# Two sequences' rotation sums, norm products and softmax scalings moved from GpSimd to VectorE, with every engine's order replanned

## The chip, the cores and the metric

The kernel runs on one core of one Trainium2 chip. Its engines are named as the profile names them: PE is TensorE (matmuls; PEld are its weight loads), DVE is VectorE, ACT is ScalarE, POOL is GpSimd, SP is SyncE, which issues most of the DMAs. Each engine works through its own instructions in the order in which they stand in its queue; semaphores make one engine wait for another. PSUM holds matmul results, SBUF everything else on the chip. The metric is the time of one execution in microseconds (us): the median of the runs shown. A line such as L1158 is a line of the kernel before; in the changed kernel lines behind L424 stand three lines higher.

## The reference

The input is eight sequences of 256 tokens with 128 channels. It goes through eight layernormed residual sublayers: an RG-LRU recurrence, local attention with a feed-forward (two depth layers), Mamba, a top-1 mixture of 32 experts, chunked attention, a top-2 mixture of 8 experts, typed attention with 16 heads, and a ternary linear layer. The change touches the second, local attention. For one depth layer, cut to what matters:

```
x = x + attention(shift_token(x));  x = x + ffn(layernorm(shift_token(x)))
def l2norm(t): return t / clip(norm(t, axis=-1), 1e-12)
def rotate_half(x): x1, x2 = split(x, 2); return concatenate([-x2, x1])
q, k, v = heads(shift_token(x) @ wqkv)              # 8 heads of 64
q, k = l2norm(q) * q_scale, l2norm(k) * k_scale
q = q * cos * scale + rotate_half(q) * sin * scale
k = k * cos / scale + rotate_half(k) * sin / scale
sim = 8 * q @ k^T                 # windows of 64, one window looked back, causal
out = softmax(sim) @ v;  attention = out @ wo
```

A rotation is thus a sum of two products with tables; the norm's reciprocal multiplies q and k; and a softmax row is divided by its sum.

## The kernel before

**Stages.** The program runs six stages one behind the other: rglru, local_mamba, moe1, chunked, moe2, typed. local_mamba (L1335) holds the local attention and the Mamba layer. `one_sequence(b)` (L1383) runs a sequence through two local blocks, adds the residual (L1388) and normalizes. `interleave` (L1470) keeps up to four sequences open at once; when sequence b is finished, `mamba_sequence` (L1223) of the same sequence follows. Its state update is, eight times for each sequence, a product (L1304), a scan (L1306) and a product (L1307) on DVE. The second group of RG-LRU sequences (4 to 7, `rglru_group`, L1005) runs beside the first local blocks, with a reciprocal (L1035), a scan (L1040) and products (L1042, L1043) on DVE and its sigmoids and exponentials on ACT.

**A local block.** `local_block` (L1172) makes the shifted input h (copies L1069 on POOL), calls the attention and then the feed-forward (L1186 to L1218). `local_qk` (L1073) computes for q (n = 0) and k (n = 1) two tiles of 128 tokens each:

- PE multiplies h with the weights into a PSUM bank `qk`; ACT squares it into `qsq` (L1085); DVE sums the squares by head into `ss` (L1086).
- DVE forms the two rotation products t1 and t2 from PSUM (L1090, L1092; 128x512 each), with the scales folded into the tables.
- POOL clips ss from below (L1097), ACT turns it into the reciprocal norm rn by a logarithm and an exponential (L1098, L1099).
- POOL adds t2 to t1 (L1105) and, for k alone, multiplies with rn (L1107). PE transposes the result into `qkt` (L1110) and ACT copies it out. For q the norm is applied later, as a scale within the softmax.

`local_attention` (L1119) then works on two halves of 128 tokens: PE writes the scores `sc`; DVE takes the negated maximum nm (L1147) and multiplies it with q's rn (L1148); ACT computes eight exponentials with their sums (L1153); DVE takes the reciprocal rc of the sums (L1157); POOL multiplies e with rc (L1158, 128x1024); PE transposes e into `pt` (L981), ACT and DVE copy it to `ptsb` (L983), and PE multiplies with v into `o`, after which `wo` follows.

**What sets the order.** A class `_Order` (L312) plans all instructions of the program before it is built. It has a table `LENGTHS`, which gives for each form of instruction the time it keeps its engine and the time until its result is there; a table `BIAS` of corrections in ns to an instruction's priority, by engine, tile name and stage (stages are numbered 1 to 6, so "DVE nm 2" is the nm operations of local_mamba on DVE); and `STAY`, which holds back an instruction that would make PE change its tile group or ACT its function table. `plan` (L612) walks through time and on each engine issues the ready instruction with the lowest corrected start; it also models that DVE and POOL operations of some forms exclude each other. `impose` (L760) then writes the result into the program as order on every engine:

```
for ring in order.values():
    for a, b in zip(ring, ring[1:]):
        self.tc.add_manual_dep(...)
```

So the order on PE, DVE, ACT, POOL and SP, in all stages, follows from these tables together with the instructions.

Of the kernel before, what the change touches and what calls it, by code (L numbers as in the profile page):

```python
# [18 lines left out]
ALU = mybir.AluOpType  # L19
# [4 lines left out]
P = 128  # L24
# [287 lines left out]
class _Order:  # L312
# [14 lines left out]
    STAY = dict(PE=80, ACT=740)  # L327
    BIAS = {
        "ACT  1": 100, "ACT  5": 585, "ACT bt 3": 5, "ACT bt 5": -775, "ACT d 2": -425, "ACT da 2": -45, "ACT e 2": -5, "ACT e 4": 965, "ACT e 6": -20,
        "ACT got 3": 575, "ACT h 2": -200, "ACT ix 4": 15, "ACT k 2": 265, "ACT lavp 2": 210, "ACT lnrs 1": -10, "ACT lnrs 2": -160, "ACT lnsq 1": -135,  # L330
        "ACT lnsq 2": 15, "ACT ot 2": 10, "ACT ptsb 2": -595, "ACT ptsb 6": -515, "ACT q 2": 20, "ACT qsq 2": 10, "ACT r 2": -5, "ACT rg 1": 10,
        "ACT rg 2": -915, "ACT rn 2": 15, "ACT rs 4": 340, "ACT rs 6": -690, "ACT s 6": 200, "ACT sakq 2": -10, "ACT sg 3": -550, "ACT sh 5": -2525,
        "ACT spe 1": -220, "ACT spt 1": -50, "ACT st 6": 100, "ACT sz 2": 280, "ACT v 2": 885, "ACT vs 4": 320, "ACT xchunked 2": 15, "ACT xs 2": -610,
        "DVE biasfull 3": -335, "DVE biaspart 3": -20, "DVE bt 5": -5, "DVE c 1": 590, "DVE centre 0": 320, "DVE d 2": 10, "DVE decaypart 4": -600,
        "DVE e 4": 570, "DVE four 4": 100, "DVE fs 4": -70, "DVE gate 4": 340, "DVE get 2": 200, "DVE got 4": 530, "DVE identb 0": -50, "DVE k 6": 500,
        "DVE lg 2": 2240, "DVE lo 4": -265, "DVE mv 4": -660, "DVE mv 5": 100, "DVE mv 6": -485, "DVE nm 2": -3975, "DVE nm 6": 4960, "DVE nth 4": -45,
        "DVE oh 2": -725, "DVE oh 5": -10, "DVE ptsb 2": -3895, "DVE ptsb 6": 895, "DVE put 4": -395, "DVE put 5": 55, "DVE q 5": -825, "DVE q 6": -475,
        "DVE rc 2": -1225, "DVE rc 6": 10, "DVE route 2": -55, "DVE s 5": 10, "DVE sares 2": 70, "DVE sel 2": -1590, "DVE sg 3": -140, "DVE sm 4": 2720,
        "DVE spl 1": -215, "DVE ss 2": 370, "DVE st 4": 85, "DVE st 6": 1645, "DVE sum 4": 170, "DVE t 2": 440, "DVE u 2": 250, "DVE vs 4": 50,
        "DVE we 4": 1425, "DVE xc 2": 460, "DVE xla 4": -15, "DVE xlocal 2": -5, "DVE xmoe 5": -200, "DVE xmoe 6": -580, "DVE xpf 4": -370,  # L340
        "DVE xrglru 2": 120, "DVE xsa 4": 80, "DVE z 4": -1990, "PE a 2": -100, "PE acc 5": 155, "PE b 2": -35, "PE bt 3": 75, "PE bt 5": 50,
        "PE cum 2": -995, "PE cum 4": -25, "PE cum 5": -615, "PE fold 2": 2915, "PE g 2": -4155, "PE gate 2": 785, "PE kps 4": 135, "PE less 2": 295,
        "PE lg 2": 1680, "PE lg 4": 50, "PE ln 2": -10, "PE o 2": 10, "PE o 6": -10, "PE pg 5": 150, "PE ps 4": -15, "PE pt 4": -130, "PE pu 3": 220,
        "PE py 3": -200, "PE py 5": 170, "PE qk 2": 25, "PE qkt 2": -720, "PE raw 2": -8675, "PE rows 2": 400, "PE sc 2": -50, "PE sc 4": 65, "PE sc 6": 5,
        "PE v 5": 290, "PE vps 2": 4075, "PE vps 4": 25, "PE wo 2": 75, "PE wo 6": -85, "PE wout 2": -115, "PE xin 2": 1180, "PE xps 2": -2540, "PE y 2": 20,
        "PE z 2": -450, "PE zt 5": 560, "PE zt 6": 25, "POOL d 2": 130, "POOL e 6": -30, "POOL got 4": -200, "POOL h 2": 370, "POOL k 5": 400,
        "POOL k 6": 850, "POOL km 6": 1240, "POOL mean 0": 1510, "POOL places 5": -200, "POOL q 6": 20, "POOL rest 4": -65, "POOL rg 1": -800,
        "POOL rg 2": -200, "POOL rot 2": -400, "POOL s 6": -750, "POOL t 2": 550, "POOL zero 0": -655, "POOL zeros 1": 385, "SP bc 2": -970, "SP cst 3": 5,
        "SP got 3": 355, "SP got 5": 350, "SP rottable 0": 80, "SP rows 4": 210, "SP rowschunked 4": -105, "SP vec 0": -830, "SP w 0": 15, "SP w 3": 115,
        "SP wattn 2": 585, "SP wffn 2": 705, "SP wlocal 0": 1175, "SP wmoe 4": 520, "SP xs 2": -105, "SP ybuf 5": -200,  # L350
    }
    LENGTHS = {
        "ACT  LoadActFuncSet  ": (1178, 1283), "ACT d Ln 128x512 128x512": (535, 640), "ACT da Exp 128x255 128x255": (398, 503),
        "ACT e Abs 128x256 128x256": (460, 565), "ACT e Exp 128x128 128x128": (420, 525), "ACT e Exp 128x256 128x256": (461, 566),
        "ACT e Exp 128x512 128x512": (527, 632), "ACT four Exp 128x2 128x2": (100, 205), "ACT got DMACopy 128x512 128x512": (454, 3611),
        "ACT h TensorCopy 64x255 64x255": (295, 400), "ACT lnrs Exp 128x256 128x256": (315, 420), "ACT ot TensorCopy 128x512 128x512": (486, 591),
        "ACT qsq Square 128x512 128x512": (494, 599), "ACT r Relu 128x256 128x256": (460, 565), "ACT rg Exp 128x1020 128x1020": (1039, 1144),
        "ACT rg Exp 128x1024 128x1024": (998, 1103), "ACT rg Ln 128x1024 128x1024": (950, 1055), "ACT rn Exp 128x16 128x16": (110, 215),
        "ACT rn Ln 128x16 128x16": (112, 217), "ACT rs Exp 128x2 128x2": (96, 201), "ACT rs Ln 128x2 128x2": (98, 203),
        "ACT sh Silu 128x512 128x512": (492, 597), "ACT v TensorCopy 128x512 128x512": (485, 590), "ACT xc Identity 128x256 128x256": (460, 565),  # L360
        "ACT xc Silu 128x512 128x512": (526, 631), "ACT xchunked TensorCopy 128x256 128x256": (263, 368), "ACT xmoe Identity 128x256 128x256": (404, 509),
        "ACT xs TensorCopy 33x256 33x256": (257, 362), "ACT xsq Square 128x128 128x128": (297, 402), "DVE biaspart TensorCopy 96x256 96x256": (197, 282),
        "DVE decay TensorScalarPtr 128x512 128x512": (508, 593), "DVE decaypart TensorCopy 128x512 128x512": (331, 416),
        "DVE four TensorScalarPtr 128x4 128x4": (76, 160), "DVE ge TensorScalarPtr 128x256 128x256": (380, 465),
        "DVE ge TensorScalarPtr 85x256 85x256": (372, 457), "DVE got TensorScalarPtr 128x128 128x128": (258, 343),
        "DVE h TensorTensor 128x256 128x256": (312, 397), "DVE hs TensorScalarPtr 128x1024 128x1024": (2189, 2274),
        "DVE hs TensorTensor 128x1024 128x1024": (1116, 1201), "DVE mv BNStatsAggregate 128x2 128x6": (82, 167),
        "DVE nm TensorTensor 128x8 128x8": (66, 151), "DVE ptsb TensorCopy 128x512 128x512": (589, 674), "DVE rc Reciprocal 128x16 128x16": (160, 245),
        "DVE rc Reciprocal 128x4 128x4": (84, 169), "DVE rc Reciprocal 128x8 128x8": (106, 191), "DVE rg TensorScalarPtr 128x256 128x256": (577, 662),
        "DVE rg TensorTensor 128x1024 128x1024": (1109, 1194), "DVE rottable TensorScalarPtr 128x256 128x256": (261, 346),  # L370
        "DVE s TensorScalarPtr 128x128 128x128": (247, 332), "DVE s TensorTensor 128x256 128x256": (323, 408),
        "DVE sm TensorReduce 128x16 128x512": (593, 678), "DVE ss TensorReduce 128x8 128x512": (594, 679), "DVE st BNStats 128x6 128x128": (197, 282),
        "DVE sum TensorReduce 128x32 128x448": (810, 895), "DVE t TensorScalarPtr 128x256 128x256": (384, 469),
        "DVE t TensorTensor 128x512 128x512": (593, 678), "DVE vec TensorTensor 128x1 128x1": (59, 144), "DVE vec TensorTensor 85x1 85x1": (59, 144),
        "DVE vs TensorCopy 128x512 128x512": (594, 679), "DVE wlocal TensorScalarPtr 128x682 128x682": (481, 566),
        "DVE x TensorScalarPtr 128x256 128x256": (368, 453), "DVE xc TensorScalarPtr 128x254 128x254": (383, 468),
        "DVE xc TensorScalarPtr 128x255 128x255": (384, 469), "DVE xla TensorScalarPtr 128x256 128x256": (442, 527),
        "DVE xlocal TensorTensor 128x256 128x256": (311, 396), "DVE xpf TensorScalarPtr 128x256 128x256": (562, 647),
# [393 lines left out]
class _Kernel:  # L772
# [293 lines left out]
    def shift(self, dst, src):  # L1066
# [3 lines left out]
        nc.gpsimd.memset(dst[64:P, 0:1], 0.0)  # L1070
        nc.scalar.copy(dst[64:P, 1:S], src[64:P, 0 : S - 1])

    def local_qk(self, l, h, w, rot, work, local, small, pools):  # L1073


        nc = self.nc
        ss = small.tile([P, 4, 8], F32, tag="ss", name="ss")
        rn = small.tile([P, 4, 8], F32, tag="rn", name="rn")
        ts = []
        for n in range(2):  # L1080
# [31 lines left out]
            if n:  # L1112
                k = dst
# [1297 lines left out]
```

## Time and profile before

| | us |
|---|---|
| median of 3 runs (lowest to highest) | 1642.47 (1641.91 to 1643.14) |
| the profiled execution | 1644.68 |
| its span | 1642.9 |

The granted clock of TensorE over the span was 0.942. By milestones in the timeline of the profiled execution: the first RG-LRU group ends at 41 us; sequence 0's first block (last addition L1218) ends at 121.2 and its second at 211.8; its residual addition (L1388) stands at 213.3 and its first Mamba scan (L1306) at 252.7. L1388 of the eight sequences stands at 213.3, 287.9, 368.4, 446.6, 526.6, 598.7, 659.5 and 719.5 us, that is 60 to 81 us apart. The last scan is at 787.4. The first mixture of experts follows, the chunked stage runs from about 850 to 1262, the second mixture of experts to about 1445 and the typed stage to the end.

How to read the lines that follow. A group line names line, engine, operation, output tile and inputs, partitions x elements and the count; behind the bar the busy time of the group in us and the mean of one instruction in ns; behind the next bar the idle time of the engine just before these instructions and who ended it. A line of waits names the waiting engine, tile and line, then the releaser, then us in total, times and the longest. A line of a stretch names its start and end. Busy time of pipelined instructions overlaps: two DVE operations of 680 ns that follow each other start 600 ns apart.

### The profile page before, as it was taken

What the parts mean: (1) busy time and instruction counts of PE and PEld (TensorE: products, weight loads), DVE (VectorE), ACT (ScalarE), POOL (GpSimd) and SP (SyncE); (2) the same over time, 40 slices, a digit from 0 to 9 for tenths busy, and PEclk for the clock granted to TensorE, in tenths of its full rate; (3) what the DMA queues carried; (4) which work ended last, traced back from release to release, by engine and by line L of the source; (5) the groups of instructions that cost most, each with busy time, mean ns of one, the idle gap of its engine ahead of it and who ended that gap; (6) DMA issues with size and microseconds to landing.
All of it is one profiled execution on the core that took longest, in us unless ns stands there. A gap on an engine that the chain in (4) does not pass through costs nothing. (4 is left out here: it accounts for less than half of the span.)

```text
span 1642.9 us, 28581 instructions
## 1 busy us (share of the span) xinstructions
PE 1417.4 (86%) x10826; PEld 909.4 (55%) x10826; DVE 1102.3 (67%) x2182; ACT 968.6 (59%) x2656; POOL 587.5 (36%) x535
## 2 busy tenths in 40 slices
PE   2688998989898887777579999999998899899997
PEld 1354554545554544334366766777675576556664
DVE  5745568898989898698545557554546333279886
ACT  3777888787978869446125545455453222167775
POOL 1334544535462523101431222212212102467774
PEclk7789999989999999779789999999998899999998
DMA  5000012121212223155430000000000130000000
GB/s 199 1 1 1 1 40 65 40 60 45 65 40 65 53 52 91 52 179 189 151 119 1 8 12 11 10 5 8 32 18 24 46 121 26 26 9 8 5 8 11
DMA packets 45113, 77.97 MB, mean 47 GB/s; under 512 B 5580, under 2 KB 21988, under 8 KB 43824
## 3 DMA queue, kind: packets, MB, share of 16 engines
q1 hardware_dynamic: 39648, 70.02, 14.0%
q0 software_dynamic: 3216, 5.07, 1.1%
q8 instruction: 85, 1.39, 0.4%
q10 hardware_dynamic: 2112, 1.05, 0.2%
q14 instruction: 52, 0.43, 0.1%
HBM read 66.87 MB, written 10.76 MB: 47 GB/s over the span
## 5 line engine op out<-in xcount | busy, mean ns | idle before, releaser
L870 PE MATMUL y<-hs,ident 128*128 128x512 f32 x256 | 139.7, 659 | 35.9 <-DVE hs L1307 35.6
L1158 POOL TENSOR_TENSOR e<-e,rc 128x1024 f32<-128x1024 f32 x32 | 78.0, 2437 | 202.7 <-DVE rc L1157 194.3
L1306 DVE TENSOR_TENSOR_SCAN hs<-da,hs 128x1024 f32<-128x1024 f32 x64 | 149.1, 2331 | 0.2
L2259 ACT ACTIVATE e<-sc,nm 128x128 f32<-128x128 f32 (+1 forms) x256 | 105.2, 427 | 46.6 <-DVE nm L2254 40.3
L1153 ACT ACTIVATE e<-sc,nm,rn 128x128 f32<-128x128 f32 x256 | 114.3, 466 | 13.8 <-DVE nm L1148 13.5
L981 PE MATMUL pt<-ident,e 128*128 128x128 f32 x768 | 114.2, 278 | 9.4 <-POOL e L1158 4.9
L1302 ACT ACTIVATE da<-d,na 128x255 f32<-128x255 f32 x256 | 109.3, 504 | 17.5 <-DVE hs L1306 13.7
L1836 POOL TENSOR_TENSOR e<-e,rc 128x512 f32<-128x512 f32 x32 | 34.0, 1064 | 219.8 <-DVE rc L1835 154.2
L981 PEld LDWEIGHTS pt<-ident,e 128*128 128x128 f32 x768 | 88.5, 141 | 42.5 <-issue 16.1
L2262 POOL TENSOR_TENSOR e<-e,rc 128x1024 f32<-128x1024 f32 x48 | 90.8, 1896 | 39.1 <-DVE rc L2261 32.1
L1105 POOL TENSOR_TENSOR t<-t,t 128x512 f32<-128x512 f32 x64 | 83.9, 1316 | 58.0 <-DVE t L1092 51.6
L1811 ACT COPY kp<-kps 128x512 f32<-128x512 f32 x128 | 74.7, 583 | 49.0 <-PE kps L870 46.4
L1658 POOL DMA_INDIRECT got<-ybuf,get x48 | 45.7, 952 | 159.2 <-DMA ybuf<-ys 97.1
L870 PEld LDWEIGHTS y<-hs,ident 128*128 128x128 f32 x256 | 48.5, 205 | 82.5 <-DVE hs L1307 54.2
L1304 DVE TENSOR_TENSOR hs<-u,bc 128x1024 f32<-128x1024 f32 x64 | 84.3, 1328 | 2.9 <-POOL u L1291 2.9
L1307 DVE TENSOR_TENSOR hs<-hs,bc 128x1024 f32<-128x1024 f32 x64 | 80.6, 1260 | 0.0
L1847 ACT COPY vs<-vps 128x512 f32<-128x512 f32 x64 | 37.4, 585 | 67.1 <-PE vps L870 53.6
L983 DVE COPY ptsb<-pt 128x512 f32<-128x512 f32 x104 | 68.8, 675 | 11.6 <-PE pt L981 9.3
L870 PE MATMUL qk<-w_local,h 128*128 128x512 f32 x128 | 69.3, 631 | 7.5 <-DVE t L1092 7.1
L870 PE MATMUL vps<-sa_vp,x_lf 128*32 128x512 f32 x512 | 68.4, 594 | 0.0
L1847 DVE COPY vs<-vps 128x512 f32<-128x512 f32 x64 | 43.3, 682 | 37.2 <-PE vps L870 25.1
L2057 DVE TENSOR_TENSOR sh<-sh,pu 128x512 f32<-128x512 f32 x32 | 22.0, 688 | 67.1 <-PE pu L870 54.0
(380 smaller groups left out, 3782.4 us busy)
## 6 DMA issues: line engine op xcount, KB each, us to landing
bc<-xs SPq DMA_DIRECT2D x128, 256.0 KB
w_moe<-in_e_dram SPq DMA_DIRECT2D x16, 768.0 KB
w_attn<-in_w_dram SPq DMA_DIRECT2D x4, 1024.0 KB
w_local<-in_w_dram SPq DMA_DIRECT2D x2, 1557.0 KB
places<-zeros SPq DMA_DIRECT2D x2, 1280.0 KB
got<-places SPq DMA_DIRECT2D x6, 256.0 KB
ybuf<-ys SPq DMA_DIRECT2D x8, 160.0 KB
x_in<-in_x_dram SPq DMA_DIRECT2D x1, 1024.0 KB
```

The costliest lines, as they stand in the source:

```text
L870: return self.nc.tensor.matmul(out, lhsT, rhs, start=start, stop=stop)
L981: self.last = self.nc.tensor.transpose(pt[:, j * P : (j + 1) * P], src[:, j * P : (j + 1) * P], self.ident)
L1105: nc.gpsimd.tensor_add(t1, t1, t2)
L1153: nc.scalar.activation(e[:, j, g, :], scs[:, j, g, :], AF.Exp, bias=nm[:, j, g : g + 1], scale=rq[:, j, g : g + 1], accum_out=sm[:, j, g : ...
L1158: nc.gpsimd.tensor_tensor(e, e, rc.unsqueeze(3).to_broadcast([P, 2, 4, P]), ALU.mult)
L1302: nc.scalar.activation(da[:, n, c, 1:S], d[:, c, 1:S], AF.Exp, scale=na[:, i : i + 1])
L1304: nc.vector.tensor_tensor(hs, u.unsqueeze(1).to_broadcast(shp), bn, ALU.mult)
L1306: nc.vector.tensor_tensor_scan(line(hs), line(da), line(hs), 0.0, ALU.mult, ALU.add)
L1307: nc.vector.tensor_tensor(hs, hs, cn, ALU.mult)
L1847: i = copy(v[:, c, :, :].rearrange("p a b -> p (a b)"), ps)
L2259: nc.scalar.activation(e[:, i, :], sc[:, i, :], AF.Exp, bias=nm[:, i : i + 1], accum_out=sm[:, i : i + 1])
L2262: nc.gpsimd.tensor_tensor(e, e, rc.unsqueeze(2).to_broadcast([P, n, keys]), ALU.mult)
```

## The change

`local_qk`, `local_attention` and `local_block` take the engine `eng` as an argument; `one_sequence` passes VectorE for sequences 0 and 1 and GpSimd for the other six. Three operations are issued on that engine: the rotation sum (4 in a block), k's product with the norm (2) and the scaling of the exponentials (2). With two blocks for a sequence that makes 32 instructions. The clipping of ss (L1097) and the copies of h stay on POOL.

The planner's tables are changed as well: `STAY` goes from 80 to 150 for PE and from 740 to 950 for ACT; nearly all entries of `BIAS` have other values, some are gone and some new; `LENGTHS` has newly measured values, mostly a few ns apart, with some entries dropped. Since the order on every engine follows from these, it is another one in all stages.

```diff
-    STAY = dict(PE=80, ACT=740)
+    STAY = dict(PE=150, ACT=950)
     BIAS = {
...
-    def local_qk(self, l, h, w, rot, work, local, small, pools):
+    def local_qk(self, eng, l, h, w, rot, work, local, small, pools):
...
-                nc.gpsimd.tensor_add(t1, t1, t2)
+                eng.tensor_add(t1, t1, t2)
                 if n:
-                    nc.gpsimd.tensor_tensor(t1, t1, rn[:, 2 + t, :].unsqueeze(2).to_broadcast([P, 8, 64]), ALU.mult)
+                    eng.tensor_tensor(t1, t1, rn[:, 2 + t, :].unsqueeze(2).to_broadcast([P, 8, 64]), ALU.mult)
...
-    def local_attention(self, l, h, w, rot, work, local, small, pools):
+    def local_attention(self, eng, l, h, w, rot, work, local, small, pools):
...
-        q, k, rn = yield from self.local_qk(l, h, w, rot, work, local, small, pools)
+        q, k, rn = yield from self.local_qk(eng, l, h, w, rot, work, local, small, pools)
...
-            nc.gpsimd.tensor_tensor(e, e, rc.unsqueeze(3).to_broadcast([P, 2, 4, P]), ALU.mult)
+            eng.tensor_tensor(e, e, rc.unsqueeze(3).to_broadcast([P, 2, 4, P]), ALU.mult)
...
-    def local_block(self, l, x, w, rot, work, local, small, pools):
+    def local_block(self, eng, l, x, w, rot, work, local, small, pools):
...
-        ot = yield from self.local_attention(l, h, w, rot, work, local, small, pools)
+        ot = yield from self.local_attention(eng, l, h, w, rot, work, local, small, pools)
...
-                    x = yield from self.local_block(l, x, w, rot, work, local, small, pools)
+                    x = yield from self.local_block(nc.vector if b < 2 else nc.gpsimd, l, x, w, rot, work, local, small, pools)
```

Of `BIAS`, some entries of the stage of the edit are these (before, then after): "DVE nm 2" -3975, -2300; "DVE ptsb 2" -3895, -6115; "DVE rc 2" -1225, -2400; "PE qkt 2" -720, -6440; "PE raw 2" -8675, -7230; "POOL t 2" 550, 2725; "POOL h 2" 370, 1290.

## The prediction

> **What bounds the kernel now.** I read the busy sums first, then busy time by stretch, then the costliest groups of the early stretch, and last its waits.
>
> ```profile
> PE 1417.4 (86%) x10826; PEld 909.4 (55%) x10826; DVE 1102.3 (67%) x2182; ACT 968.6 (59%) x2656; POOL 587.5 (36%) x535
> ...
> 42.00:120.00 78.00, 57.29 (x313) 34.10 (x312) 48.08 (x82) 56.03 (x135) 23.88 (x28) 0.80 0.00 1
> 120.00:253.00 133.00, 117.13 (x815) 71.63 (x814) 81.27 (x140) 107.94 (x303) 70.51 (x79) 0.99 0.04 13
> 253.00:660.00 407.00, 353.04 (x2020) 209.01 (x2019) 365.02 (x445) 331.38 (x868) 178.90 (x146) 0.97 0.22 58
> 660.00:796.00 136.00, 97.29 (x398) 52.38 (x396) 108.58 (x119) 64.68 (x134) 27.77 (x20) 0.84 0.48 162
> 860.00:1262.00 402.00, 393.31 (x4508) 278.60 (x4500) 226.87 (x722) 196.92 (x461) 84.56 (x92) 1.00 0.04 11
> 1445.00:1620.00 175.00, 170.93 (x1574) 102.85 (x1572) 149.66 (x360) 126.84 (x579) 126.38 (x80) 1.00 0.02 6
> ```
>
> The first line is the whole span. The others are stretches: start and end, length, then busy time (instructions) of PE, weight loads, DVE, ACT and POOL, the granted clock, DMA share and GB/s. The sums hide four regimes. 42–253 holds the first three sequences of local blocks, the two edited ones among them: PE 73%, then 88%; DVE is busy 129.4 of 211 us and idle 81.6. From 253 to 660 the Mamba scans run and DVE is the bound (365.0 of 407). After 860 PE is, at 98% in the chunked and the typed stage. All moved work lies before 253; only the first regime changes by the code, the others by order alone.
>
> ```profile
> L1105 POOL TENSOR_TENSOR t<-t,t 128x512 f32<-128x512 f32 x32 | 43.4, 1360 | 40.1 <-DVE t L1092 35.9 <-PE wo L870 1.6 <-PE gate L870 1.0
> L1158 POOL TENSOR_TENSOR e<-e,rc 128x1024 f32<-128x1024 f32 x12 | 23.0, 1920 | 52.9 <-DVE rc L1157 52.7
> L1107 POOL TENSOR_TENSOR t<-t,rn 128x512 f32<-128x512 f32 x16 | 16.9, 1064 | 9.1 <-ACT rn L1099 8.8
> ...
> L1092 DVE TENSOR_TENSOR t<-qk,rot 128x512 f32<-128x512 f32 x32 | 21.7, 680 | 0.0
> L1035 DVE RECIPROCAL rg<-rg 128x1024 f32<-128x1024 f32 x1 | 6.6, 6553 | 0.0
> ```
>
> These are groups between 42 and 260: busy sum, mean ns of one, idle time before and who ended it. The three POOL lines are what moves; POOL mostly waits for DVE there, so it is a link in a chain, not a bound. The DVE line is the nearest price of a moved 128x512 operation.
>
> ```profile
> POOL t L1107 <- ACT rn L1099: 7.5, 3, 4.7
> PEld qkt L1110 <- POOL t L1105: 2.5, 3, 1.1
> PEld qkt L1110 <- POOL t L1107: 1.8, 4, 0.8
> PEld pt L981 <- POOL e L1158: 1.7, 3, 0.7
> PE pt L981 <- POOL e L1158: 0.7, 2, 0.5
> PE qkt L1110 <- POOL t L1105: 0.5, 2, 0.3
> ```
>
> Waits from 42 to 254: who waited for whom, total us, times, longest. With 0.4 us more on another name PE waited 7.6 us in all for the three POOL lines, in six blocks. That is the most a faster link can return there directly. The first row is the wait that will stand in DVE's queue.
>
> **The change part by part.**
>
> *Removed from POOL.* Four blocks (two sequences, two layers) hold 16 rotation sums, 8 products with the norm and 8 scalings. At the undisturbed durations that the timeline shows (1.27, 1.04, 1.90 us) that is 20.3 + 8.3 + 15.2 = 43.8 us. POOL is no bound before 253 (94.4 of 211 us), so the sum is worth 0 by itself; POOL's ss maxima and copies of h only come sooner.
>
> *Added to DVE.* L1092's 680 ns starts every 0.60 us in the timeline, since ends overlap the next start. 24 operations of 128x512 at 0.60 are 14.4 us; 8 of 128x1024 at about 1.14 (the cadence of L1307, 1.22 us alone) are 9.1: 23.5 us, 11.75 for each sequence. All instructions of DVE ordered ahead of the first scan, priced by the rows of before, grow from 163.3 to 186.2 us. I cost it at 0, covered by DVE's 81.6 idle us. If the cover is gone for sequence 0's share, the price is 11.75 x 129.4/211 (the busy share) = +7.2 us; that is one upper end.
>
> *The chain of sequence 0.* Its blocks end at 121.2 and 211.8, the first scan starts at 252.7, and from there the DVE-bound pipeline follows, so what sequence 0 gains or loses is carried on. Per softmax half the scaling falls from 1.90 to 1.22 us, and the hand-over from the reciprocal (80.89 to 80.97, later 89.70 to 89.77) stays on one engine: about -1.0 at most. Per last k tile, a sum and a product fall from 1.27 + 1.04 to 2 x 0.68: about -1.0 to -1.3. By place in the new order of DVE:
> - Layer 0, first half: its max reduction now goes ahead of the RG-LRU group's 6.55 us reciprocal (L1035), but the product of nm and rn, which the exponentials need, goes behind it: no gain.
> - Layer 0, second half: the scaling stands behind another half's maximum, L1042 and a product with rn. One such row is 1.22: some 2.5 us later at one half, equal at the other; the wo product that follows also waits for ACT and PE. I take 0.
> - Layer 1, q and k (122 to 141): DVE's queue grows from 15.6 to 19.2 us of work in an 18.1 us segment that had 2.5 idle. POOL paced the same segment, nearly without a break from 133.8 to 142. Even.
> - Layer 1, softmax halves: -1.0 and -1.6 (there POOL's scaling also stood behind copies of h).
>
> I take -2.5 for the chain. The low end is 4/6 of the 7.6 us of waits, -5.1; the top end is all of the 7.5 us of the rn wait turned into a stall of DVE, +7.5. I stay nearer to the low end because the order puts rn of k on ACT two table loads (1.28 us each) earlier than before, so the longest of those waits, 4.7 us at 65.6, should shrink.
>
> *The new wait on DVE.* k's product waits for ACT's rn at the head of an in-order queue. Behind it in the first block are the RG-LRU chain of sequences 4 to 7 and the next sequence's ss; ACT's squares and PE's qk banks wait for those. Its price is the +7.5 above, not a second term.
>
> *Sequence 1.* It takes the same 11.75 us of DVE. PE was 88% busy between 120 and 253 and sequence 1 joins the pipeline only when sequence 0's scans are done (its last addition at 287.9, the next at 368.4): 0, and +2 at most, if its last half slips into the scans.
>
> *The pipeline from 253 to 796.* DVE's queue behind sequence 0's last addition is priced at 1074.4 us before and 1076.2 after: 0, +1.8 at the top.
>
> The shared use of SBUF is where a rule and a row can be set beside each other. L1158 took 1.92 us on average here and, beside the scans, 2.75 (20 of them between 260 and 800, 54.9 us); the moved ones run where DVE's two-input rows are few, so I count no lock time removed. The Trainium skill's "Perfetto Trace Analysis", section "Optimizing Scalar/DVE Operations", speaks against this change: work shifted between GpSimd and VectorE might not help, since they share a read port. By that rule the move is worth nothing and the sum would be -1.5 instead of -4.0. The section "Identifying the Most-Contended Engine" of the same page adds that the busiest engine is to be relieved; if DVE counted as that one all along, sequence 0's whole 11.75 us would be added, +10 in all. The row against it is DVE's 81.6 idle us in the stretch concerned.
>
> *The replanned rest.* The planner's priorities and durations change, so every engine's order does. ACT has one table load more, 1.28 us, in stretches where PE or DVE leads: 0, at most +1.3. PE's changes of tile group fall from 90 to 86 in the chunked and 106 to 98 in the typed stage, and rise from 200 to 206 in the local one. The weight-load waits put down to "issue" bound one: 8.6 us in 17 cases before qkt, 0.5 each, and 0 if hidden; twelve fewer where PE is the bound are 0 to -6. Near the groups of 0.2 (6.6 us in 34 before the typed scores), less the six more, I take -1.5. In DMA queues SP now issues scales and local weights ahead of the tables (first inputs still first) and w_ffn ahead of w_attn near 748, where the last scans cover both: 0. POOL's gathers between the first MoE and the chunked stage get two additions between them: 0 to +2, taken 0, since later gathers have slack. What an order may spoil unseen I bound by PE's idle time: the PE-bound stages left 8.7 + 4.1 us, the stretch 796–860 23. I allow -4 to +5 around the -1.5.
>
> **Sum.** -2.5 (chain) + 0 (DVE's added work) - 1.5 (order) = -4.0 us. The profiled execution took 1644.68 us (span 1642.9, 1.8 around it), which becomes 1640.7; it stood 2.2 above the median of the runs, 1642.47, so the prediction is 1638.5.
>
> **Rivals.**
> - *DVE becomes the link that is late* (slower). The rn wait and the reciprocal L1035 stand in the queue that now carries the scalings and sums. For: 3 waits of 7.5 us, DVE gapless from 124.8 to 133.5, 19.2 us of work for 18.1. Against: 81.6 idle us and rn ordered earlier. Price: +7.5 without the chain's -2.5 and with -1.5 for the order: +6, 1648.5. It decides once more than 4 us of stall lands where DVE had no idle time.
> - *The latencies were hidden* (no change). For: PE waited only 7.6 us for POOL, ACT is 81% and PE 88% busy from 120 to 253. Against: PE's 20.7 idle us from 42 to 120, when few sequences are open. The chain is 0 and the order -1.5 or 0: 1641 to 1642.5.
> - *A larger gain*: the chain reaches -5.1 and the order -5.5: 1631.9. For: the waits sum to that; against: two halves sit behind other DVE work.
> - *The move does not take effect*: excluded, the order has exactly 32 instructions less on POOL and 32 more on DVE.
>
> **How the numbers follow.** 0.2% of 1642.47, 3.3 us, is about what a measurement of this kernel tells from no change. My forecast (-4, give or take 2.5) has 0.33, the larger gain 0.17, hidden latencies 0.20, the late DVE 0.30, a third of it beyond +6 when the order spoils something else too. Faster: 0.17 + two thirds of my forecast, 0.22, plus a little from the hidden case with a good order, 0.04 = 0.43. Same: one third of the forecast (0.11) and 0.10 of the hidden case = 0.21. Slower: 0.30 and 0.06 of the hidden case with a bad order = 0.36. The range reaches from the larger gain's place less some 4 us, 1628, to the late DVE's plus 3.5, 1652. The forecast alone is 1636 to 1641.
>
> **What would show it.** Right: the three lines at 0.68 and 1.22 us on DVE under the two sequences; x of sequence 0 before 120 and 210, the first scan some 2.5 us before 252.7, the last at about 785 instead of 787.4; no wait of DVE on rn above 2 us. Wrong: a DVE wait for rn of 4 us or more with the RG-LRU chain behind it, the first scan after 255, or a stage after 796 that differs by more than 4 us, which would be the order alone.

## The result and the profile after

The changed kernel is slower: 1657.92 us median (1655.30 to 1660.75, 4 runs) against 1642.19 (1638.17 to 1643.14, 4 runs) beside it, a ratio of 1.0098 with a 95% interval of 1.0074 to 1.0121. That is some 16 us more, where 4 us less were forecast, and it lies outside the range. The profiled span went from 1642.9 to 1659.0 us.

What the edit does to the two engines is as forecast. The first line of the page of after, and the groups of the moved lines between 42 and 262 us (columns as before; lines stand three higher):

```profile
PE 1428.8 (86%) x10826; PEld 910.5 (55%) x10826; DVE 1127.1 (68%) x2214; ACT 973.9 (59%) x2657; POOL 545.0 (33%) x503
```

```profile
L1102 DVE TENSOR_TENSOR t<-t,t 128x512 f32<-128x512 f32 x16 | 10.7, 686 | 0.1
L1155 DVE TENSOR_TENSOR e<-e,rc 128x1024 f32<-128x1024 f32 x8 | 9.9, 1240 | 0.2
...
L1104 DVE TENSOR_TENSOR t<-t,rn 128x512 f32<-128x512 f32 x8 | 6.4, 812 | 0.7 <-ACT rn L1096 0.6
```

POOL lost 42.5 us, DVE gained 24.8 (43.8 and 23.5 forecast), and DVE waited for rn only 0.6 us in all. But PE, which has the same 10826 instructions, is busy 11.4 us longer.

Where the time went, by points that both profiles have:

| | before, us | after, us | lag of after |
|---|---|---|---|
| first softmax exponential (L1153) | 75.4 | 81.0 | +5.6 |
| sequence 0, end of first block (L1218) | 121.2 | 126.5 | +5.3 |
| sequence 0, L1388 | 213.3 | 220.7 | +7.3 |
| first scan of sequence 0, 1, 2 (L1306) | 252.7, 330.5, 417.7 | 262.4, 345.1, 420.3 | +9.8, +14.6, +2.6 |
| last Mamba output (L1313) | 793.7 | 794.5 | +0.8 |
| first copy of kp, chunked stage (L1811) | 851.3 | 853.6 | +2.3 |
| last x_pf, end of chunked stage (L1979) | 1264.3 | 1272.6 | +8.3 |
| first maximum of the typed stage (L2254) | 1444.9 | 1452.8 | +7.9 |
| end | 1642.9 | 1659.0 | +16.1 |

The two edited sequences come late, but the lag is gone by the last scan. The loss is made behind them, in stages whose code is the same: 1.5 us in the first mixture of experts, 6.0 in the chunked stage, 8.2 in the typed stage, and 0.4 back in the second mixture. The busy time by stretch shows the chunked and then the typed stage, first of before, then of after (columns as in the stretches of before):

```profile
851.30:1264.30 413.00, 403.24 (x4580) 286.26 (x4579) 232.16 (x736) 203.74 (x480) 90.22 (x99) 1.00 0.04 12
...
1444.90:1642.90 198.00, 182.30 (x1684) 110.66 (x1682) 160.15 (x389) 133.50 (x604) 131.63 (x84) 0.98 0.02 7
```

```profile
853.60:1272.60 419.00, 405.68 (x4580) 285.67 (x4579) 232.73 (x737) 205.25 (x480) 89.41 (x98) 0.99 0.04 12
...
1452.80:1659.00 206.20, 189.95 (x1684) 111.78 (x1682) 161.45 (x389) 134.37 (x604) 132.07 (x84) 0.98 0.02 6
```

The typed stage has the same 1684 matmuls and the same clock (0.98), and PE is busy 7.7 us longer with them. In the chunked stage PE is busy 2.4 us longer, and the rest of the 6 us is idle time.

### The profile page after: what moved, and what is told of

Read it like the earlier page. It is cut to its first block, busy times and chain, and to the rows that moved or that the text cites. A ratio compares the mean times of both kernels' runs of the same rounds, so it can differ in the third digit from the quotient of the medians.

```text
span 1659.0 us, 28568 instructions
## 1 busy us (share of the span) xinstructions
PE 1428.8 (86%) x10826; PEld 910.5 (55%) x10826; DVE 1127.1 (68%) x2214; ACT 973.9 (59%) x2657; POOL 545.0 (33%) x503
## 3 DMA queue, kind: packets, MB, share of 16 engines
q10 hardware_dynamic: 2112, 1.05, 0.2%
## 4 chain that ended last, share of the span: by engine, by line
PE 57%; DVE 21%; ACT 10%; issue 7%; POOL 3%; DMA 1%; another core or an unknown queue 0%; ACTq 0%; SPq 0%; DVEq 0%; POOLq 0%
PE sc L867 8%; PE vps L867 8%; PE kps L867 7%; PE out L867 4%; DVE hs L1303 4%; PE pt L978 4%; PE pu L867 3%; PE pg L867 3%; DVE hs L1304 3%; PE o L867 3%; DVE hs L1301 3%; ACT e L1150 2%; PE hps L867 2%; PE y L867 2%; PE py L867 1%
## 5 line engine op out<-in xcount | busy, mean ns | idle before, releaser
L978 PE MATMUL pt<-ident,e 128*128 128x128 f32 x768 | 118.0, 281 | 12.6 <-DVE e L1155 3.8
L1155 POOL TENSOR_TENSOR e<-e,rc 128x1024 f32<-128x1024 f32 x24 | 61.9, 2580 | 175.7 <-DVE rc L1154 175.6
L1299 ACT ACTIVATE da<-d,na 128x255 f32<-128x255 f32 x256 | 108.7, 503 | 17.9 <-DVE hs L1303 16.5
L978 PEld LDWEIGHTS pt<-ident,e 128*128 128x128 f32 x768 | 87.4, 142 | 55.2 <-issue 26.9
L2259 POOL TENSOR_TENSOR e<-e,rc 128x1024 f32<-128x1024 f32 x48 | 90.8, 1897 | 43.7 <-DVE rc L2258 37.7
L1301 DVE TENSOR_TENSOR hs<-u,bc 128x1024 f32<-128x1024 f32 x64 | 80.2, 1268 | 3.5 <-POOL u L1288 3.4
L1102 POOL TENSOR_TENSOR t<-t,t 128x512 f32<-128x512 f32 x48 | 63.0, 1317 | 39.9 <-DVE t L1089 38.6
L867 PE MATMUL sc<-msk,identb 128*128 128x512 bf16 (+2 forms) x224 | 48.7, 358 | 22.5 <-ACT e L1150 22.4
```

Source lines behind the costliest of these rows:

```text
L867: return self.nc.tensor.matmul(out, lhsT, rhs, start=start, stop=stop)
L978: self.last = self.nc.tensor.transpose(pt[:, j * P : (j + 1) * P], src[:, j * P : (j + 1) * P], self.ident)
L1299: nc.scalar.activation(da[:, n, c, 1:S], d[:, c, 1:S], AF.Exp, scale=na[:, i : i + 1])
L1301: nc.vector.tensor_tensor(hs, u.unsqueeze(1).to_broadcast(shp), bn, ALU.mult)
L2259: nc.gpsimd.tensor_tensor(e, e, rc.unsqueeze(2).to_broadcast([P, n, keys]), ALU.mult)
```

## The experiments

Two theories stood against each other: the loss is the replanned order of the later stages (the order theory), or it starts with DVE being late in sequence 0. The kernels ran on several chips, and the kernel before took between 1629 and 1646 us on them, so each ratio is against the kernel before on the same chip.

### The edit with the old tables, and the tables without the edit

```diff
 # e1: the changed functions, tables of before
-    STAY, BIAS, LENGTHS of after
+    STAY, BIAS, LENGTHS of before
 # e2: the functions of before, tables of after
-                    x = yield from self.local_block(nc.vector if b < 2 else nc.gpsimd, l, x, ...)
+                    x = yield from self.local_block(l, x, ...)
```

> The edit (32 operations on DVE in sequences 0 and 1) with the priorities, durations and thresholds of before. The order of PE behind the Mamba stage is then word for word that of before, so all that differs is made before about 800 us. Order theory (the loss lies in the replanned chunked and typed stages): within 3 us of before, last Mamba output within 2 us of 793.3. Rival (the edit itself: DVE is late in sequence 0, and what is lost there is carried to the end): 5 to 10 us slower than before, last Mamba output near 800. A third reading (the edit alone gains what I forecast): 2.5 us faster.

> The kernel before with the changed tables alone; the 32 operations stay on POOL. Order theory: 13 to 17 us slower than before, like the changed kernel, with the chunked stage 5 to 6 us and the typed stage 8 us longer. Rival (the edit itself): within 5 us of before, 8 or more faster than the changed kernel.

Measured: e1 1636.44 us, ratio 1.0060 (1.0038 to 1.0082); e2 1672.54 us, ratio 1.0270 (1.0245 to 1.0295). e1 alone would have spoken for the rival, and e2 overshot both theories. The profile of e2 shows where: the first scan stands at 272.0 us and the last Mamba output at 823.7, some 30 us later than in either kernel, and only then come the typed stage's 207.4 us. So the priorities of the local and Mamba stage depend on which engine does the moved work: 1.006 and 1.027 are the two mismatched pairs. In e1 the order of the stages behind the Mamba stage is that of before, and its last Mamba output stands at 799.6 us; its loss is made ahead of that. Neither run says what the matched pair is worth.

### Only the sums and products, or only the scalings, with the old tables

```diff
 # h1: scalings alone
-                eng.tensor_add(t1, t1, t2)
+                nc.gpsimd.tensor_add(t1, t1, t2)
-                    eng.tensor_tensor(t1, t1, rn[...], ALU.mult)
+                    nc.gpsimd.tensor_tensor(t1, t1, rn[...], ALU.mult)
 # h2: sums and products alone
-            eng.tensor_tensor(e, e, rc..., ALU.mult)
+            nc.gpsimd.tensor_tensor(e, e, rc..., ALU.mult)
```

> Tables of before; only the 8 scalings of the exponentials go to DVE, sums and products stay on POOL. If it is the scalings that wait in DVE's queue, it loses as much as all 32 together did, 6 to 7 us against before; if the sums and products fill DVE between 120 and 142, it is within 2 us of before.

> Tables of before; only the 16 rotation sums and 8 products with the norm go to DVE, the scalings stay on POOL. If these make DVE the late link, 6 to 7 us slower than before; if it is the scalings, within 2 us of before or faster by up to 2.

Measured: h1 1650.69 us, ratio 1.0015 (0.9998 to 1.0033), not clear of no change; h2 1690.33 us, ratio 1.0250 (1.0225 to 1.0274). h2 is far worse than all 32 operations together, which no reading of the operations' own cost allows: 24 operations of 0.6 us cannot lose 41 us where 32 lose 7 to 10. Its first scan is at 273.5 us and its last Mamba output at 836.5, and PE's order differs up to the last third of the Mamba stage. So the loss belongs to the plan that the planner finds for this mixture and not to the operations. Which wait makes the 41 us is not shown.

### Early order and late order taken apart

Since the tables act by stage, a kernel can have one set up to the Mamba stage (stages 0 to 2) and the other behind it.

```diff
+    STAY_LATE = ...; LENGTHS_LATE = ...   # of the other kernel; BIAS by stage likewise
-        return self.LENGTHS.get(self.form(i)) or self.length(i)
+        lengths = self.LENGTHS if self.stage[i] < 3 else self.LENGTHS_LATE
+        return lengths.get(self.form(i)) or self.length(i)
-                        far = self.STAY.get(e, 0) if ...
+                        far = (self.STAY if self.stage[item[1]] < 3 else self.STAY_LATE).get(e, 0) if ...
```

> The kernel before, profiled beside the others, to compare stages on one chip: chunked stage 405 to 413 us, typed stage 198 us, last Mamba output between 786 and 794 us.

> The changed kernel beside the others. Typed stage 206 us against 198. If the 6 us that the chunked stage lost between the first two profiles belong to its order, it is again 5 to 6 us longer than before's; if they were stalls of that execution, it is within 2 us of before's, and the kernel 9 to 12 us slower than before in all.

> The changed kernel, with the tables of before for all stages behind the Mamba stage: order as changed up to there, word for word that of before from the chunked stage on. Order theory: 8 us faster than the changed kernel by the typed stage alone, and within 3 us of before. Rival (the early stages lose it): within 3 us of the changed kernel.

> The kernel before up to the end of the Mamba stage, with the sums, products and scalings on POOL, and the changed tables for all later stages: their order is that of the changed kernel. If the moved operations are worth nothing and the late order is the whole loss, it is 10 to 13 us slower than before, as the changed kernel was beside it on one chip (11.4). If the moved operations carry a part of the loss, it is less by that part.

Measured, on one chip: before 1630.38, after 1641.78 (ratio 1.0071, 1.0052 to 1.0089), and with the new early and the old late order 1630.11, ratio 0.9997 (0.9985 to 1.0008). On another chip, the old early and the new late order: 1661.38 against 1644.43, ratio 1.0092 (1.0070 to 1.0114). The four corners agree: with the late order of before the kernel is level, whichever engine does the moved work, and with the changed late order it loses what the changed kernel lost. Order theory held; the edit together with the early order that belongs to it costs and brings nothing that these runs can tell (-2.4 to +1.3 us).

The typed stage and the chunked stage in the first of these, which has after's order up to the Mamba stage's end:

```profile
849.10:1255.40 406.30, 399.47 (x4580) 284.48 (x4579) 231.78 (x736) 203.55 (x480) 90.04 (x99) 1.00 0.04 12
1429.00:1627.10 198.10, 182.43 (x1684) 110.80 (x1682) 160.04 (x389) 133.24 (x604) 131.51 (x84) 0.97 0.02 7
```

198.1 us again, with PE busy 182.4 as before. The kernel before on this chip had 406.7 and 198.1 us in the two stages.

### One stage's priorities at a time

```diff
 # e3: of BIAS, the keys that end in 6 are those of after; all else is before
 # e4: of BIAS, the keys that end in 4 are those of after; all else is before
 # k1: after; BIAS, STAY and LENGTHS of the typed stage are those of before
 # m1: after up to stage 3; BIAS, STAY and LENGTHS of before from stage 4 on
```

> The kernel before; of the changed tables only the priorities of the typed stage. Nothing in front of the typed stage is ordered differently. Order theory: 8 us slower (typed stage 206 instead of 198 us), with PE's idle time in the stage the same within 1 us and the loss in the slots where PE goes from one kind of matmul to another. Rival (a late arrival from the stages before, or the edit): no change within 2 us.

> The kernel before; of the changed tables only the priorities of the chunked stage. Order theory: 5 us slower, made between 850 and 1268 us, nothing lost later. Rival: no change within 2 us, the loss of the changed kernel in this stage then comes from elsewhere (the thresholds for changing the tile group or the function table, the durations).

> The changed kernel with the tables of before for the typed stage alone: order as changed up to there. Typed stage 198 instead of 206 us, time 8 us below the changed kernel; what is left against the kernel before, 3 to 4 us, is the order of the first mixture of experts (60 to 62 us from the last Mamba output to the first copy of kp, 57 to 58 before).

> The changed kernel up to and with the first mixture of experts, the tables of before from the chunked stage on. If the order within that mixture is worth the 3.7 us that separate the profiles there, it is 3 to 5 us slower than before (the same early order with the old mixture was level with before), and from the last Mamba output to the first copy of kp pass 60 to 61 us. Rival (half-clock periods of TensorE that fell there by chance): within 1.5 us of before.

Measured: e3 1636.53 us, ratio 1.0059 (1.0037 to 1.0080), typed stage 206.1 us: the 8 us come from the typed stage's priorities alone.

```profile
1421.90:1628.00 206.10, 190.12 (x1684) 111.45 (x1682) 160.91 (x389) 133.99 (x604) 132.03 (x84) 0.98 0.02 7
```

k1 confirms it from the other side: its typed stage, with the order of before, takes 199.8 us at a granted clock of 0.96, and it is 1651.12 us against 1645.90, ratio 1.0038 (1.0023 to 1.0053).

e4 lost more than its theory allowed: 1646.93 against 1629.41 us, ratio 1.0120 (1.0092 to 1.0149), with a chunked stage of 423.8 us. These priorities without the thresholds and durations that were set with them make a worse order than either kernel has, so this run does not price the chunked order of after. The profiles of the others do, and they depend on the chip. Where the kernel before takes 1629 to 1630 us its chunked order takes 404.7 to 406.7 us, and after's 405.4 to 409.2; where the kernel before takes 1642 to 1646 us, before's order takes 412.4 to 414.2 and after's 417.6 to 420.0. The waits of PE in that stage: one line of before, then the longest of the changed kernel, then of e2, which has the changed order there but ran on the other kind of chip:

```profile
PE out L870 <- issue: 2.0, 6, 0.4
```

```profile
PE out L867 <- issue: 4.3, 12, 1.0
PE zt L1794 <- DVE z L1788: 3.3, 2, 2.8
PE hps L867 <- DVE x_la L1904: 2.4, 3, 0.9
```

```profile
PE zt L1794 <- DVE z L1788: 2.8, 1, 2.8
PE out L1980 <- DVE x_pf L1976: 1.1, 1, 1.1
```

Twelve waits of up to 1.0 us for which the profile names no releaser are there on the one and absent on the other. With 2.0 us of them in the matmuls of "out" before and 4.3 after, the changed order meets more of them. What they are stays open; so does the cause of the 3 to 8 us that the chunked stage cost on such chips.

m1 took 1647.94 us against 1644.43, ratio 1.0018 (1.0004 to 1.0031), and 58.5 us from the last Mamba output to the first copy of kp, where before took 57.6 and after 59.1 (58.9 to 61.7 in the six others with the new order there). By the ratio the order of the first mixture is thus worth 3.0 us, with an interval from 0.7 to 5.1 that also holds the rival's 1.5. TensorE's granted clock differed as well: 0.79 in that stretch of the new-early, old-late kernel, 0.77 in before and 0.72 to 0.77 where the order was new. Some 8 us of the typed stage and 3 of the first mixture make up the 11.4 us that the changed kernel lost on the chip of the new-early, old-late kernel.

### Sequence 0's late softmax

In after the first block is late at one visible place. DVE's timeline in before, then in after (start, duration, engine, line):

```profile
66.12 6.55 DVE L1035 RECIPROCAL rg<-rg 128x1024 f32<-128x1024 f32 x1
72.62 1.23 DVE L1147 TENSOR_REDUCE nm<-sc 128x8 f32<-128x1024 f32 x1
73.76 0.68 DVE L1031 TENSOR_SCALAR rg<-rg 128x1024 f32<-128x1024 f32 x1
74.36 0.16 DVE L1148 TENSOR_TENSOR nm<-nm,rn 128x8 f32<-128x8 f32 x1
```

```profile
73.22 1.22 DVE L1144 TENSOR_REDUCE nm<-sc 128x8 f32<-128x1024 f32 x1 [2.39 <-PE sc L867]
74.37 6.54 DVE L1032 RECIPROCAL rg<-rg 128x1024 f32<-128x1024 f32 x1
80.83 0.10 DVE L1145 TENSOR_TENSOR nm<-nm,rn 128x8 f32<-128x8 f32 x1
```

The reciprocal starts 8.3 us later than before, and it now stands between the maximum and the product that the exponentials need. Of the 8.3 us, 3.5 go to the maximum that now stands ahead of it: 2.4 us in which DVE was idle until PE had the scores (the bracket in its line), and 1.1 us of its own.

```diff
         order, _ = self.plan()
+        dve = order["DVE"]
+        at = ...   # the last Reciprocal of tile rg in local_mamba
+        dve[at], dve[at + 1] = dve[at + 1], dve[at]
```

> The changed kernel with one swap in DVE's order: the small product of nm and rn of sequence 0's first softmax half goes ahead of the RG-LRU group's reciprocal of 6.5 us. If that reciprocal is what makes sequence 0 late: its exponentials start near 75.6 instead of 81.0, its first block's end moves from 126.5 to about 122, the first scan from 262 to 258. Whether it is carried on: if the pipeline carries all of it the time falls by 4 to 5 us; if the pipeline has slack the last Mamba output stays within 1.5 us and the time is the same.

Measured: 1641.24 us beside the changed kernel's 1641.78 on that chip; ratio to before 1.0063 (1.0049 to 1.0078). The exponentials did start at 74.0 instead of 78.5 us (the new-early, old-late kernel beside it, same order so far). But the block's wo addition came at 108.3 against 108.1, so nothing arrived earlier. The next thing was late instead, the scaling of the same half, now DVE's own (this kernel has the line numbers of before):

```profile
72.83 6.54 DVE L1035 RECIPROCAL rg<-rg 128x1024 f32<-128x1024 f32 x1
79.29 1.16 DVE L1037 TENSOR_TENSOR rg<-rg 128x1024 f32<-128x1024 f32 x1
...
83.29 0.17 DVE L1157 RECIPROCAL rc<-sm 128x8 f32<-128x8 f32 x1
...
87.35 0.16 DVE L1148 TENSOR_TENSOR nm<-nm,rn 128x8 f32<-128x8 f32 x1
87.43 1.22 DVE L1158 TENSOR_TENSOR e<-e,rc 128x1024 f32<-128x1024 f32 x1
```

The exponentials end at 77.6, but rc stands behind the reciprocal until 83.3 and the scaling behind other work until 87.4. On POOL, before, the scaling started at 81.0. So the place is shown; that the early part as a whole is worth nothing at the end is shown by the new-early, old-late kernel.

### The two halves of a score product

In the typed stage a unit's scores begin with two products over 64 rows each (L870, sc<-km,q), one for each half of PE's rows, and mostly two more for the decay. PE's busy time in that stage by group, in before, in after, and in the kernel p1 below:

```profile
L870 PE MATMUL sc<-km,q 64*128 64x512 f32 x184 | 51.9, 641 | 0.0
```

```profile
L867 PE MATMUL sc<-km,q 64*128 64x512 f32 x184 | 57.5, 641 | 0.0
```

```profile
L873 PE MATMUL sc<-km,q 64*128 64x512 f32 x184 | 51.9, 641 | 0.0
```

The count and the mean are the same, the sum is not: in after some of them no longer run at the same time. The timeline of PE shows which, first a unit of before, then one of the five of after:

```profile
1497.85 1.13 PE L870 MATMUL sc<-km,q 64*128 64x512 f32 x4
1498.81 0.38 PE L870 MATMUL sc<-decay,onesb 64*128 64x512 bf16 x2
1499.13 0.39 PE L870 MATMUL sc<-msk,identb 128*128 128x256 bf16 x2
```

```profile
1513.92 1.12 PE L867 MATMUL sc<-km,q 64*128 64x512 f32 x2
1514.97 0.71 PE L867 MATMUL wo<-w,ot 128*128 128x128 f32 x4
1515.62 0.69 PE L867 MATMUL sc<-km,q 64*128 64x512 f32 x1
1515.62 0.39 PE L867 MATMUL sc<-decay,onesb 64*128 64x512 bf16 x1
1516.15 0.59 PE L867 MATMUL sc<-km,q 64*128 64x512 f32 x1
1516.58 0.38 PE L867 MATMUL sc<-decay,onesb 64*128 64x512 bf16 x1
1516.89 0.39 PE L867 MATMUL sc<-msk,identb 128*128 128x256 bf16 x2
```

Before, the four products (two of each half) and the decay take 1.28 us. After, the wo products stand between the halves, and the two parts take 1.05 and 1.27 us: 1.04 us more for each unit.

```diff
         order, _ = self.plan()
+        # typed stage: sc, wo, wo, sc  becomes  wo, wo, sc, sc
+        pe[n : n + 3] = pe[n + 1], pe[n + 2], pe[n]
```

> The changed kernel with one correction in PE's order: in five units of the typed stage two wo products stand between the two halves of a score product (64 rows each); they are put ahead of both. If the halves, when they stand side by side, run at the same time and otherwise one behind the other, each unit gains about 1.0 us: 5 us off the typed stage (206 to 201) and off the time. Rival (the loss lies in the number of changes between kinds of matmul, 201 against 179): at most 5 changes fewer, below 1 us.

Measured: typed stage 202.8 us instead of 206.2 (206.1 to 207.8 in all profiles with the changed order); time 1654.02 us against 1645.90 of the kernel before, ratio 1.0057 (1.0035 to 1.0078). The changed kernel was not timed on that chip, so the gain is read from the stage. The sum of all starts-to-next-starts of the 64-row products, worked out from PE's timeline, is 53.8 us in before, 59.0 in after and 53.8 in p1: the halves are worth 5.2 us, as the theory said. Of these 1.8 us are lost again, mostly because the wo products now stand where their operands are late:

```profile
PE wo L873 <- DVE vm L2223: 1.4, 5, 0.3
```

The other part of the 8 us lies, by the same sums, in the matmuls over the whole array: 106.2 us before and 108.7 after, 0.5 of it idle time. The 32-column products took 33.1 and 33.2 us, and PE's gaps were 10.7 and 11.0 us in all. The visits to whole-array matmuls rose from 80 to 101, but that these are the cause is not shown: p1 has 96 visits and 110.5 us, 10.3 of them idle against 8.9 in after.

The Trainium skill's "TensorE: Matmul & The Clock Gate", section "Part 3: Packing small matmuls — row/col tiling", describes that matmuls on different row groups of the array run at the same time, with starts about 4 ns apart. These traces agree, with 7 ns between the two starts of an undisturbed pair. What they add is that two products over the whole array between the two halves take that away, at 1.04 us for each unit.

## Why the prediction was wrong

- **Prices of the moved operations: right.** 686, 812 and 1240 ns, against 0.68 and 1.22 us; the 812 are seven products of 0.68 and one of 1.72 us.
- **"The chain of sequence 0", -2.5 us: wrong in sign.** The step that failed is "Layer 0, first half ... no gain": it was costed as if the reciprocal stood where it had stood. DVE reached it 8.3 us later: sums and products stood ahead of it, and so did the maximum, for which DVE had to wait until PE had the scores. The first half became 5.6 us later. Layer 1, called even for q and k and -2.6 for the halves, lost another 2 to 3 us (the block ends are +5.3 and +8.3).
- **"What sequence 0 gains or loses is carried on": wrong, and it saved the term.** The lag of +9.8 at the first scan and +14.6 at the second is +2.6 at the third. L1388 of sequences 2 to 7 stands 3.6, 0.5, 1.1, 2.0, 6.3 and 3.8 us later, and the last Mamba output 0.8. What took up the lag is not shown; DVE's busy share of 90% between 253 and 660 left some 40 us of room. The early part is worth 0 by the new-early, old-late kernel (0.9985 to 1.0008), which is also what the rule set beside the sum would give; no run tests the reason that the rule gives, the shared port. That is the rival "latencies were hidden" for the edit, if not for the reason it gave.
- **The rival "DVE becomes the link that is late": its place was right, its wait was not.** DVE was late by the reciprocal and by its own queue, not by rn (0.6 us). A lag of that size was there at the first scan (+9.8) and gone at the last Mamba output (+0.8).
- **"The replanned rest", -1.5 us, -4 to +5: this decided it.** It was +15 in these two profiles (from +0.8 at the last Mamba output to +16.1 at the end) and 11.7 between the changed and the new-early, old-late kernel on one chip. The failed step is the price of PE's order: the planner's changes of tile group were counted as falling from 106 to 98 in the typed stage, and I took that for a gain. By the trace the visits to a kind of matmul rose from 179 to 201 there. The 106 and 98 are twice the visits to 32-column products in the traces (53 and 49), so it seems that the count held these alone; five pairs of 64-row products were split, which cost 5.2 us, and nothing in the sum stood for that. The rest of the typed stage's 8 us and the chunked stage's share stay open. I bounded what an order can spoil by PE's idle time, 4.1 us in the typed stage. But the loss was no idle time: PE stayed busy, 190.0 instead of 182.3 us, on the same matmuls.

## What to carry to other kernels

A list scheduler's order is part of the kernel: when its tables change, cost every stage that it reorders, not the edited one, and do it by counting in the new order which matmuls still stand side by side on separate parts of the array. A busy engine is no bound on what its order can cost; at 98% busy an order can hold 5 us of work that ran at the same time in another. And priorities tuned for one placement of work say nothing of another: two of the mismatched kernels here (h2 and e2) lost 2.5 and 2.7%, the whole change 0.7 to 1.0%.

## What the runs showed of the hardware

The same order does not take the same time through the Mamba stage. The kernels e3 and before have one order up to the typed stage, and their last Mamba output stood at 786.1 and 793.7 us. The busy time by stretch from 245 to 370 us, of before and of e3 (the granted clock is the third number from the end):

```profile
245.00:370.00 125.00, 108.57 (x566) 64.83 (x564) 109.51 (x128) 101.60 (x267) 56.69 (x45) 0.93 0.20 54
```

```profile
245.00:370.00 125.00, 106.76 (x614) 63.39 (x612) 115.28 (x132) 103.58 (x272) 57.40 (x46) 1.00 0.23 56
```

The clock was halved in periods of 3.4 us or a multiple; three fell into this stretch in before and none in e3, with PE busy 108.6 and 106.8 us. It is not the chip: e4 ran on the chip of e3, with the same order up to the chunked stage, and had the clock at 0.93 in this stretch and its last Mamba output at 793.4 us. The Trainium skill's "TensorE: Matmul & The Clock Gate", section "Part 1: The HAM clock gate (the "warmup" mystery)", says that the activity window is free-running, so that it depends on its phase where a change of clock falls; the traces fit that, though no run here shows the phase itself. One profile therefore can't tell 4 us in such a stage, and only the repeated timings settled what the early order is worth.
